# A sparse graph layer on one core: forms spread one to a block, three more units with a kept tile, short rows of A, and stores issued together with loads

## The chip, the cores and the metric

One core of a Trainium2 chip runs the kernel in one launch. The metric is the device time in microseconds (us) of one execution. The core has a matrix engine (PE; its weight loads are PEld), a vector engine (DVE), an activation engine (ACT), GpSimd (POOL) and SyncE (SP). Every engine works through its own queue of instructions in order. DMAs are issued from the queues of SP, ACT and POOL, and 16 DMA engines carry them out.

## The reference

`x` is 8 x 4096 x 256, `adj` is 4096 x 4096 (about 0.4% of its entries are nonzero, the low-numbered rows and columns most often), `W` is 256 x 256, all float32.

```python
HW = einsum('bnf,fo->bno', x, W)
A = relu((adj + adj.T) * 0.5)
D = sum(A, axis=1)
r = where(D > 0, D ** -0.5, 0)
L = eye(N) - r[:, None] * A * r[None, :]
out = relu(einsum('nm,bmo->bno', L, HW))
return layernorm(x + out, axis=-1)      # eps 1e-5, no scale or shift
```

## The kernel before

The work has two stages. The first makes a symmetric A in memory (`a_dram`), the degrees, the scaled products `g = r * (x W)` (`g_dram`, one row of 2048 floats, 8 KB, for each node, all eight batches side by side), and lists of which rows matter for which columns. The second, the gather stage, multiplies only the listed rows.

**First stage.** A is cut into 8 x 8 blocks of 512 x 512; A's 32 row groups have 128 rows each. The loop runs over rows `i` of blocks and, in each, over `j >= i`; a block off the diagonal handles (i,j) and (j,i) together. Per block: `load_adj` (SP queue, four buffers), transposes on PE and adds on DVE (`symmetrise`, L424 and L428), then ReLU on ACT, a sum per 64 columns on DVE (`part`, L433) and a store from the ACT queue (`keep`). After a row of blocks `degrees` gives r for its four row groups (L450 to L454). Beside a block's transposes PE does *forms*: `form(m, known)` loads x for row group m (two halves, `xin`), transposes it (L522) and multiplies by W (L533). A form is *known* when r of its rows is there: it is scaled and stored at once. The last ten row groups (`HOLD`) are formed *early*, kept in SBUF and scaled and stored by `release` later. From block row 4 on, the x loads of known forms go through the POOL queue. `multiply` adds each g's product with the first 128 columns of A to the result of the first row group (`lead`, L491). How many forms a block gets is set by a running `credit`: 1 for a block off the diagonal, 0.5 for one on it, doubled from row 4 on; in the last two block rows only the block on the diagonal gets one. Some blocks so get two forms and others none.

**Lists.** A unit u is a pair of row groups 2u+1 and 2u+2 (block 0 and block 1; the last unit has one). For each of the 4096 rows m a four-bit pattern says which of the four 64-column halves of the unit's columns have a nonzero there. `KINDS` are the patterns that have lists of their own (1, 2, 4, 8: one half; 3 and 12: one whole block; 5, 10, 9, 6: two halves of different blocks), and 0 stands for all the rest, treated as full. `CAPS[u]` gives the number of 128-row tiles of each kind. `patterns` makes the pattern; `count` (PE) and `place` (DVE) give each row a slot; `count_rest` and `place_rest` place what is left over; `spread` and `collect` turn slots into index lists, and `index` turns them into row numbers of `g_dram` (`gi`) and of a view of `a_dram` (`ai`, L385). The first four units of `SEQ` get theirs in the first stage, at times set in `due`; `spread` and `collect` are done there for the first two. In units in `HUB` the first 128 rows of g are not listed: they stay in an SBUF tile (`g_hub`), and only their part of A is loaded (L810).

**Gather stage.** For each unit in the order of `SEQ`, `steps_of` gives steps of one or two tiles. For each tile POOL issues two indirect DMAs: 128 pieces of A (`ga`, L815: 128 columns, or 256 when the tile touches both blocks) and 128 rows of g (`g`, L828, into a ring of 12 tiles, which is refilled when a step has used a tile). PE multiplies them into PSUM (L1033), four chunks of 512 columns, two passes each. Each block has four PSUM banks (tags b0 and b1). When a block is complete, `finish` has ACT evict it (L684), DVE add x (L694) and take mean and variance (L703 to L722); `normalise` (L727) follows later and then the store. Two of the b0 banks serve for the matmuls of `lists`, one step after block 0 of a unit is complete; DVE has to read them (L369, L370, L185 to L190) before the next unit can use these banks. The order on the queues is written out by hand: `queue(engine)` ties an instruction behind the last one of its engine, and `after(n, fn)` runs `fn` once steps worth n have passed (a step of two halves or one full block counts 2). x for a unit's two row groups is loaded on the ACT queue (`residuals`), 10 into the unit.

In `finish`, `rest` runs 1 after the block, and within it:

```python
def end():
    in_turn(normalise, i, z, mv, rstd)

after(3, end)
```

Of the kernel before, what the change touches and what calls it, by code (L numbers as in the profile page):

```python
# [9 lines left out]
F32 = mybir.dt.float32  # L10
# [13 lines left out]

OFFERS = [
# [9 lines left out]
SEQ = [1, 2, 3, 4, 5, 6, 7, 0, *range(8, 16)]  # L35

HUB = {0, 1, 3, 6, *range(8, 15)}
# [4 lines left out]
    [1, 3, 3, 2, 2, 1, 2, 2, 1, 1, 3],  # L42
    [1, 3, 3, 3, 2, 1, 1, 1, 1, 1, 2],
    [1, 3, 3, 2, 2, 2, 1, 1, 1, 1, 2],
    [1, 3, 3, 2, 2, 1, 1, 1, 1, 1, 2],
    [1, 3, 3, 2, 2, 1, 1, 1, 1, 1, 1],
# [13 lines left out]
def kernel(  # L60
# [28 lines left out]
    P = 128  # L89
# [15 lines left out]
    mid = KINDS.index(4), KINDS.index(5)  # L105
# [259 lines left out]
    def index(u, pl):  # L365
        t = tiles[u]

        low = ipool.tile([P, tmax], F32, tag="low", name=f"low_{u}")
        nc.vector.tensor_copy(low[:, :t], pl[:, 1, :])  # L369
        nc.vector.scalar_tensor_tensor(low[:, :t], pl[:, 0, :], float(P), low[:, :t], ALU.mult, ALU.add)  # L370
        gi = ipool.tile([P, tmax], U32, tag="gi", name=f"gi_{u}", bufs=3)
        nc.vector.tensor_scalar(gi[:, :t], low[:, :t], float(N), None, ALU.add)

        ai = ipool.tile([P, tmax], U32, tag="ai", name=f"ai_{u}", bufs=3)
        m0, m1 = first[u][mid[0]], first[u][mid[1]]
        if blocks(u) == 1:
            m0 = m1 = t
        for ts, n, k in (
            (slice(0, m0), NB, 2 * u + 1),
            (slice(m0, m1), NB, 2 * u + 2),  # L380
            (slice(m1, t), NU, u),
        ):
            if ts.start == ts.stop:
                continue
            nc.vector.tensor_scalar(  # L385
                ai[:, ts], low[:, ts], float(n), float(N * n + k), ALU.mult, ALU.add
            )
        plan[u] = gi, ai
        yield
# [9 lines left out]
    with (  # L399
# [173 lines left out]
        credit = 0.0  # L573
# [37 lines left out]

        for i in range(NS):
            diag = stat1.tile([P, A, P], F32, tag="diag", name=f"diag_{i}")
            for j in range(i, NS):
                tij = load_adj(i, j)
                tji = load_adj(j, i) if j > i else tij
                parts = [(i, j, tij, tji)] + ([(j, i, tji, tij)] if j > i else [])
                parts = [(p, spool.tile([P, A, S], F32, tag="sym", name=f"sym_{p[0]}_{p[1]}")) for p in parts]
                credit += (1.0 if j > i else 0.5) * (1 if i < 4 else 2)
                beside = [multiply(*args) for args in waiting]  # L620
                waiting.clear()
                products = len(beside)

                some = i < NS - 2 or i == j
                while some and credit >= 1.0 and (known or early):
                    beside.append(form(known.pop(0), True, i >= 4) if known else form(early.pop(0), False))
                    credit -= 1.0
                    some = i < NS - 2
                credit = min(credit, 1.0)
                for p, sym in parts:  # L630
                    for _ in symmetrise(*p, sym):
                        pass
                if i == NS - 1:


                    release_all(i - 1)
                    beside = beside[products:] + beside[:products]
                for n, b in enumerate(beside):
                    with tc.issue_after(done_pe[-1]) if i == NS - 1 and n < 2 else nullcontext():
                        for _ in b:  # L640
                            pass
                for (rows, cols, _, _), sym in parts:
                    keep(rows, cols, sym, diag)
                run_due()
            degrees(i)
            diags[i] = diag
            if i != NS - 2:
                release_all(i)
            known += range(i * A, min((i + 1) * A, NB - HOLD))
            if i == 1:  # L650
                for n, u in enumerate(SEQ[:2]):
                    patterns(u)
                    due += [[2 + n, count_place, (u,)], [4 + n, count_place_rest, (u,)]]
                due.sort(key=lambda d: d[0])
            elif i == 2:
                for n, u in enumerate(SEQ[2:4]):
                    patterns(u)
                    due.append([1 + n, count_place, (u,)])
                due.append([3, count_place_rest, (SEQ[2],)])
            elif i < 5 and i > 2:  # L660

                pieces = spread_early(SEQ[i - 3])
                for n in range(5):
                    due.append([1 + n // 2, next, (pieces, None)])
                due.append([4, collect_index, (SEQ[i - 3],)])
        run_due(True)
# [58 lines left out]
    def normalise(i, z, mv, rstd):  # L725
        for b in range(B):
            nc.vector.tensor_scalar(  # L727
                z[:, b, :],
                z[:, b, :],
                mv[:, b, 0:1],  # L730
                rstd[:, b : b + 1],
                ALU.subtract,
                ALU.mult,
            )
        nc.sync.dma_start(out[:, i * P : (i + 1) * P, :].rearrange("b p f -> p b f"), z)

    a_rows = a_dram.rearrange("j (c q) -> (j c) q", q=P)
    a_pairs = a_dram.rearrange("j (c q) -> (j c) q", q=2 * P)

# [29 lines left out]
    with (  # L769
# [3 lines left out]
    ):  # L773
        ring = [
# [3 lines left out]
        hub = gath.enter_context(tc.tile_pool(name="hub", bufs=1)).tile([P, G], F32, name="g_hub")  # L778
# [11 lines left out]
            "pool": mybir.EngineType.Pool,  # L790
        }
# [6 lines left out]
        def gather(n):  # L798
# [4 lines left out]
            both = len(targets(u, kind)) == 2  # L803
            at = apool.tile([P, 2 * P], F32, tag="a", name=f"ga_{u}_{t % tmax}")
# [9 lines left out]
            with queue("pool"):  # L814
                nc.gpsimd.indirect_dma_start(  # L815
                    out=at if both else at[:, :P],
                    out_offset=None,
                    in_=a_pairs if both else a_rows,
# [89 lines left out]
        def finish(i):  # L908

            if i == NB - 1:  # L910
                finish_last(i)
                return
# [3 lines left out]
            def rest():  # L916
# [6 lines left out]
                def end():  # L923
                    in_turn(normalise, i, z, mv, rstd)

                after(3, end)
# [3 lines left out]
        def residuals(rows):  # L930
# [61 lines left out]

        finish(0)
        side = None
        for q, (u, step) in enumerate(steps):
            new = q == 0 or steps[q - 1][0] != u
            last = q + 1 == len(steps) or steps[q + 1][0] != u
            if new:
                after(6, prepare, u)
                if q > 0:  # L1000
                    after(10 if u != SEQ[-1] else 4, residuals, range(2 * u + 1, 2 * u + 1 + blocks(u)))
# [9 lines left out]
            work = [(b, rows, *got[u, t]) for m in range(2) for k, t in step for b, rows in targets(u, k)[m : m + 1]]  # L1011
# [9 lines left out]
            for b, rows, at, gt in work:  # L1021
# [5 lines left out]
            for c in range(G // S):  # L1027
                for (b, rows, at, gt), new_rows in zip(work, fresh):
                    both = any(len(targets(u, k)) == 2 for k, t in step)
                    off = b * P if both else 0  # L1030
# [13 lines left out]
            run_later(sum(1 + (rows == slice(0, P)) for _, rows, _, _ in work))  # L1044
# [14 lines left out]
    with tc.If(short > 0):  # L1059
        with (  # L1060
# [4 lines left out]
            for i in range(NB):  # L1065
# [19 lines left out]
                normalise(i, z, mv, inverse_root(i, var, stat))  # L1085

# [27 lines left out]
```

## Time and profile before

| | |
|---|---|
| three runs | 1518.22, 1521.61, 1522.28 us; median 1521.61 |
| profiled execution | 1521.9 us, its span (first to last instruction) 1520.2 us, granted PE clock 0.982 |
| PE, DVE, POOL, ACT busy | 1437.9, 987.0, 693.6, 372.3 us |
| moved by DMA | 564.49 MB, 371 GB/s on average |
| L1033, products of gathered tiles | 2872 passes, 807.1 us busy; 176 more with the kept tile, 77.3 us |
| L828 and L815, the gathers | 268 each; 12.5 and 10.9 us from issue to landing |
| L735, stores of the result | 31 of 1 MB, 25.1 us from issue to landing |

The busy time of PE is modelled from the starts of matmuls, so a busy PE can still be short of its peak. The DMA share in the views is the mean busy share of the 16 DMA engines, and can stand slightly above 1. In brackets behind a row stands the idle time ahead of it and what ended it.

### The profile page before, as it was taken

How to read it: one execution, taken by the hardware profiler on the slowest of the kernel's cores; microseconds unless marked ns; L12 is line 12 of the kernel's file. 1: busy time of each engine (PE TensorE's matmuls, PEld its weight loads, DVE VectorE, ACT ScalarE, POOL GpSimd, SP SyncE). 2: the span in 40 equal slices, each digit the busy share in tenths (PEclk: the TensorE clock that was granted, in tenths of full speed). 3: DMA queues.
4: the chain of work that ended last, by engine and by line, in shares of the span. 5: the costliest groups of instructions: out<-in, count | busy, mean ns of one | idle time of the engine just before them, and what ended most of it. 6: DMA issues, size and time to landing. Idle time of an engine off the chain costs nothing.

```text
span 1520.2 us, 19332 instructions
## 1 busy us (share of the span) xinstructions
PE 1437.9 (95%) x6440; PEld 767.5 (50%) x6440; DVE 987.0 (65%) x3015; ACT 372.3 (24%) x462; POOL 693.6 (46%) x1051
## 2 busy tenths in 40 slices
PE   6999999989989989999999998999999999999994
PEld 5878877767767764433343333343433333333331
DVE  6576578898646362155659669579037888899533
ACT  3555554545434451010100100100010111001111
POOL 3002010010302225776767666666666767666652
PEclk9999999989999999999999999999999999999998
DMA  9999999999879998999999999999989999999995
GB/s 355 352 366 400 395 377 361 357 377 346 343 256 365 325 386 352 390 419 413 374 410 390 400 405 367 385 407 383 386 310 407 349 397 404 409 390 375 378 397 192
DMA packets 216713, 564.49 MB, mean 371 GB/s; under 512 B 16550, under 2 KB 104918, under 8 KB 180134
## 3 DMA queue, kind: packets, MB, share of 16 engines
q0 software_dynamic: 54224, 304.94, 50.6%
q1 hardware_dynamic: 93472, 126.89, 24.0%
q10 hardware_dynamic: 68912, 131.37, 22.8%
q8 instruction: 53, 0.87, 0.2%
q14 instruction: 52, 0.43, 0.1%
HBM read 443.61 MB, written 136.34 MB: 382 GB/s over the span
## 4 chain that ended last, share of the span: by engine, by line
PE 65%; DMA 17%; DVE 8%; issue 5%; ACT 2%; POOL 1%; ACTq 0%; SPq 0%; DVEq 0%; POOLq 0%
PE py L1033 45%; DMA g<-g_dram,gi 10%; PE pg L533 9%; PE lead L491 5%; DMA a_dram<-sym 4%; PE tr L424 3%; DVE sym L428 3%; PE xtr L522 3%; DVE part L433 2%; DMA ga<-a_dram,ai 2%; DMA xin<-in_x_dram 1%; ACT sym L432 1%; DMA adj<-in_adj_dram 1%; POOL ga L815 1%; PE lists L357 1%
## 5 line engine op out<-in xcount | busy, mean ns | idle before, releaser
L1033 PE MATMUL py<-g,ga 128*64 128x512 f32 (+1 forms) x2872 | 807.1, 597 | 16.4 <-DMA g<-g_dram,gi 14.2
L1033 PEld LDWEIGHTS py<-g,ga 128*64 128x64 f32 (+1 forms) x2872 | 293.8, 151 | 516.6 <-issue 487.2
L828 POOL DMA_INDIRECT g<-g_dram,gi x268 | 303.8, 1133 | 201.9 <-DMA g<-g_dram,gi 78.4
L815 POOL DMA_INDIRECT ga<-a_dram,ai x268 | 294.1, 1097 | 105.9 <-issue 77.7
L684 ACT ACTIVATE y<-py,minus_r 128x512 f32<-128x512 f32 x120 | 82.5, 687 | 799.7 <-PE py L1033 736.6
L694 DVE TENSOR_TENSOR xr<-xr,y 128x2048 f32<-128x2048 f32 x31 | 71.1, 2294 | 295.1 <-ACT y L684 294.5
L533 PE MATMUL pg<-w_sb,xt 128*128 128x256 f32 x1024 | 232.3, 385 | 5.2 <-ACT xt L523 5.2
L428 DVE TENSOR_TENSOR sym<-tr,adj 128x512 f32<-128x512 f32 x256 | 163.4, 682 | 101.5 <-PE tr L424 84.7
L533 PEld LDWEIGHTS pg<-w_sb,xt 128*128 128x128 f32 x1024 | 195.8, 194 | 33.5 <-ACT xt L523 5.6
L433 DVE TENSOR_REDUCE part<-sym 128x32 f32<-128x2048 f32 x64 | 145.4, 2278 | 63.2 <-ACT sym L432 63.2
L424 PE MATMUL tr<-ident,adj 128*128 128x128 f32 x1024 | 139.5, 287 | 28.7 <-DVE sym L428 14.6
L453 POOL TENSOR_TENSOR r<-e,neg_half 128x4 f32<-128x4 f32 x8 | 8.3, 1040 | 321.7 <-DVE e L452 239.6
L432 ACT ACTIVATE sym<-sym 128x2048 f32<-128x2048 f32 x64 | 122.6, 1916 | 128.0 <-DVE sym L428 109.4
L424 PEld LDWEIGHTS tr<-ident,adj 128*128 128x128 f32 x1024 | 119.9, 147 | 58.4 <-DVE sym L428 27.0
L522 PE MATMUL xtr<-ident,xin 128*128 128x128 f32 x512 | 73.7, 292 | 17.8 <-DVE sym L428 16.6
L703 DVE BATCH_NORM_STATS2 stats<-xr 128x6 f32<-128x256 f32 x256 | 87.0, 412 | 1.1
L727 DVE TENSOR_SCALAR xr<-xr,mv,root 128x256 f32<-128x256 f32 x248 | 84.2, 410 | 0.1
L491 PE MATMUL lead<-gt,strip 128*128 128x512 f32 x176 | 83.0, 598 | 0.0
L523 ACT COPY xt<-xtr 128x512 f32<-128x512 f32 x128 | 68.6, 591 | 48.1 <-PE xtr L522 47.3
L543 ACT ACTIVATE gt<-pg,r 128x512 f32<-128x512 f32 x88 | 60.6, 689 | 75.0 <-PE pg L533 72.3
L522 PEld LDWEIGHTS xtr<-ident,xin 128*128 128x128 f32 x512 | 60.8, 149 | 34.1 <-DVE sym L428 26.3
L1033 PE MATMUL py<-g_hub,ga 128*128 128x512 f32 x176 | 77.3, 592 | 0.0
(142 smaller groups left out, 836.8 us busy)
## 6 DMA issues: line engine op xcount, KB each, us to landing
adj<-in_adj_dram SPq DMA_DIRECT2D x64, 1024.0 KB, 10.6
a_dram<-sym ACTq DMA_DIRECT2D x64, 1024.0 KB, 9.4
out_dram<-xr SPq DMA_DIRECT2D x31, 1024.0 KB, 25.1
xr<-in_x_dram ACTq DMA_DIRECT2D x29, 1024.0 KB, 26.2
xin<-in_x_dram SPq DMA_DIRECT2D x44, 512.0 KB, 11.9
g_dram<-gt ACTq DMA_DIRECT2D x22, 1024.0 KB, 7.7
xin<-in_x_dram POOLq DMA_DIRECT2D x20, 512.0 KB, 5.8
g_dram<-held ACTq DMA_DIRECT2D x10, 1024.0 KB, 10.8
```

Of the source, the lines that this page charges most:

```text
L424: ins = nc.tensor.transpose(pt[:, c * P : (c + 1) * P], tji[:, c, a * P : (a + 1) * P], ident)
L428: nc.vector.tensor_add(sym[:, a, :], pt, tij[:, a, :])
L432: nc.scalar.activation(sym, sym, AF.Relu, scale=0.5)
L433: nc.vector.tensor_reduce(part[:, i * A : (i + 1) * A, j * S // Q : (j + 1) * S // Q], sym.rearrange("p a (c q) -> p a c q", q=Q), AX.X, A ...
L491: nc.tensor.matmul(lead[c], lhsT=strip, rhs=g[:, c * S : (c + 1) * S], start=not done, stop=len(done) == NB - 1, skip_group_check=True,)
L522: nc.tensor.transpose(pt[:, k, c, :], xin[b // H][:, b % H + k, c * P : (c + 1) * P], ident)
L533: ins = nc.tensor.matmul(pg[:, k * FO : (k + 1) * FO], lhsT=xt[:, b + k, c, :], rhs=w_sb[:, c, :], start=(c == 0), stop=(c == FC - 1),)
L703: nc.vector.bn_stats(stats[:, b, :], z[:, b, :])
L727: nc.vector.tensor_scalar(z[:, b, :], z[:, b, :], mv[:, b, 0:1], rstd[:, b : b + 1], ALU.subtract, ALU.mult,)
L815: nc.gpsimd.indirect_dma_start(out=at if both else at[:, :P], out_offset=None, in_=a_pairs if both else a_rows, in_offset=bass.IndirectOff ...
L828: nc.gpsimd.indirect_dma_start(out=gt, out_offset=None, in_=g_dram, in_offset=bass.IndirectOffsetOnAxis(ap=gi[:, t : t + 1], axis=0), boun ...
L1033: nc.tensor.matmul(py[2 * u + 1 + b][c][rows, :], lhsT=at[:, off + rows.start : off + rows.stop], rhs=gt[:, c * S : (c + 1) * S], start=ne ...
```

## The change

1. *Forms.* `credit` goes. One early form is placed ahead of the loop, and then `quota(i, j)` gives each block one form, except diagonal blocks of rows 0 to 3, which get none.
2. *Lists in the first stage.* Instead of two units after block row 1 and two after row 2, one unit each starts after rows 1, 2, 3 and 4; the left-over rows of the fourth are placed in the gather stage, as before.
3. *Hub.* Units 2, 4 and 5 join `HUB`; each gives up one gathered tile (unit 2 one of kind 0, unit 4 one of kind 12, unit 5 its one of kind 6). The hub tile's place in SBUF moves ahead of the ring.
4. *Short rows.* For kinds 1, 2, 4 and 8 only the 64 columns in question are fetched from A (256 bytes a row in place of 512); `index` makes the numbers kind by kind.
5. *Order.* Unit 0 comes after unit 9 instead of after unit 7.
6. *Stores and loads.* `normalise` follows directly in `rest`. The store is put off: `exchange` issues the oldest finished store on SP together with the x load of one row group on ACT, at 6 and at 12 into each unit (2 and 4 in the last).

```diff
-SEQ = [1, 2, 3, 4, 5, 6, 7, 0, *range(8, 16)]
-HUB = {0, 1, 3, 6, *range(8, 15)}
+ALONE = {1, 2, 4, 8}
+SEQ = [*range(1, 10), 0, *range(10, 16)]
+HUB = {*range(7), *range(8, 15)}
 CAPS = [
...
-    [1, 3, 3, 2, 2, 1, 2, 2, 1, 1, 3],
+    [1, 3, 3, 2, 2, 1, 2, 2, 1, 1, 2],
     [1, 3, 3, 3, 2, 1, 1, 1, 1, 1, 2],
-    [1, 3, 3, 2, 2, 2, 1, 1, 1, 1, 2],
     [1, 3, 3, 2, 2, 1, 1, 1, 1, 1, 2],
+    [1, 3, 3, 2, 2, 1, 1, 1, 1, 0, 2],
...
-        for ts, n, k in (
-            (slice(0, m0), NB, 2 * u + 1),
-            (slice(m0, m1), NB, 2 * u + 2),
-            (slice(m1, t), NU, u),
-        ):
...
+        for k, kind in enumerate(KINDS):
+            if not CAPS[u][k]:
+                continue
+            ts = slice(first[u][k], first[u][k] + CAPS[u][k])
+            if kind in ALONE:
+                n, at = N // Q, 2 * (2 * u + 1) + kind.bit_length() - 1
...
+            nc.vector.tensor_scalar(ai[:, ts], low[:, ts], float(n), float(N * n + at), ALU.mult, ALU.add)
...
-        credit = 0.0
+        def quota(i, j):
+            if i in (2, 3) and j == i:
+                return 0
+            return int(j > i or i > 3)
...
+        for _ in form(early.pop(0), False):
+            pass
         for i in range(NS):
...
-                while some and credit >= 1.0 and (known or early):
-                    beside.append(form(known.pop(0), True, i >= 4) if known else form(early.pop(0), False))
-                    credit -= 1.0
+                for _ in range(quota(i, j)):
+                    if known:
+                        beside.append(form(known.pop(0), True, i >= 4))
+                    elif early:
+                        beside.append(form(early.pop(0), False))
...
-            if i == 1:
-                for n, u in enumerate(SEQ[:2]):
-                    patterns(u)
-                    due += [[2 + n, count_place, (u,)], [4 + n, count_place_rest, (u,)]]
...
+            if i in (1, 2, 3, 4):
+                u = SEQ[i - 1]
+                patterns(u)
+                due.append([2, count_place, (u,)])
+                if i < 4:
+                    due.append([4, count_place_rest, (u,)])
...
-                    out=at if both else at[:, :P],
-                    in_=a_pairs if both else a_rows,
+                    out=at if both else at[:, :Q] if half else at[:, :P],
+                    in_=a_pairs if both else a_halves if half else a_rows,
...
-                def end():
-                    in_turn(normalise, i, z, mv, rstd)
-                after(3, end)
+                in_turn(normalise, i, z, mv, rstd)
+                finished.append((i, z))
...
-        def residuals(rows):
+        def exchange(rows):
+            if finished:
+                with queue("sp"):
+                    store(*finished.pop(0))
             for i in rows:
                 with queue("act"):
                     xr[i] = residual(i, nc.scalar)
...
-                    after(10 if u != SEQ[-1] else 4, residuals, range(2 * u + 1, 2 * u + 1 + blocks(u)))
+                after(6 if u != SEQ[-1] else 2, exchange, rows[:1])
+                if q > 0:
+                    after(12 if u != SEQ[-1] else 4, exchange, rows[1:])
```

## The prediction

> **What bounds it now.** I read the stages first (windows view: length, busy time of PE, PEld, DVE, ACT and POOL with instruction counts, granted clock, DMA share, GB/s).
>
> ```profile
> 0.00:222.00 222.00, 202.68 (x1167) 169.99 (x1168) 141.56 (x173) 116.78 (x141) 28.56 (x403) 0.99 1.03 373
> 222.00:383.50 161.50, 145.06 (x785) 112.47 (x783) 140.03 (x393) 75.20 (x84) 8.10 (x17) 0.96 0.99 362
> 383.50:546.00 162.50, 150.83 (x815) 117.46 (x816) 88.74 (x128) 73.58 (x88) 38.80 (x63) 0.96 0.88 325
> 546.00:595.50 49.50, 44.14 (x133) 24.22 (x132) 15.73 (x29) 16.56 (x16) 15.47 (x22) 0.93 0.93 367
> 595.50:905.00 309.50, 309.50 (x1213) 119.37 (x1214) 186.98 (x705) 24.43 (x36) 216.76 (x197) 1.00 1.01 400
> 1139.00:1338.00 199.00, 199.00 (x852) 76.34 (x851) 162.57 (x636) 22.83 (x34) 135.15 (x119) 1.00 1.00 392
> ```
>
> Rows i=0,1 of the first stage (to 222) are bound by transfers (share 1.03). Rows 2,3 (to 383.5) nearly so, with VectorE at 140 of 161.5. Rows 4 to 6 (to 546) leave transfers idle (0.88). In the gather stage (595.5 to 1507) PE and the DMA engines are both full. Which leads? I counted the matmuls of L1033 off against the steps of each unit. A pass of 512 columns is due 0.43 us (the chain has PE lead L491 x72 in 30.9 us); two half-width passes into different column halves share one slot. That gives 2000 slots, 857 us, in a stage of 911.7. The other 54.7: the lists' matmuls 17.6; waits for gathers 25.3 (13.5 in units 6, 7 and 0, between 917 and 1045; 11.8 in unit 15); one wait for VectorE 2.2; the rest, small, 9.6. The chain of waits (start, length) leaves PE for gathers in those places only:
>
> ```profile
> 854.20 50.40 PE py L1033 x184
> ...
> 904.87 12.37 DMA g<-g_dram,gi
> ...
> 1456.57 13.38 DMA g<-g_dram,gi
> ```
>
> So PE leads, and transfers add 25 us. Then the boundary between two units, on the timeline (start, length):
>
> ```profile
> 1230.49 2.29 DVE L694 TENSOR_TENSOR xr<-xr,y 128x2048 f32<-128x2048 f32 x1 [5.41 <-ACT y L684]
> 1233.55 0.95 PE L357 MATMUL lists<-val,hot 128*128 128x28 bf16 x32
> 1238.62 0.17 DVE L369 COPY low<-lists 128x14 f32<-128x14 f32 x1
> 1239.43 0.31 DVE L385 TENSOR_SCALAR ai<-low 128x5 uint32<-128x5 f32 x3
> 1241.14 0.52 DVE L189 TENSOR_TENSOR pos_k<-incl_k,lists 128x352 f32<-128x352 f32 x1
> 1242.13 2.84 DVE L727 TENSOR_SCALAR xr<-xr,mv,root 128x256 f32<-128x256 f32 x8
> ```
>
> VectorE reads the lists out of two of the four b0 banks, and only then normalises. Unit 10's first step begins at 1241.3 and needs the first of these banks for its third column chunk, 1.7 us later; L189 frees it at 1241.7. The spare time is 1.4 us. At unit 12 it is negative already, and PE waits:
>
> ```profile
> 1341.53 1.94 PE L1033 MATMUL py<-g,ga 128*64 128x512 f32 x8 [2.01 <-DVE pos_k L189]
> ```
>
> **First stage: forms and lists.** All 32 forms stay. A form is 8.7 us of PE (xtr x16 1.75, pg x32 6.91), its product 3.4. Rows 0,1: one form goes ahead of the loop and K0 leaves block (1,1); the bytes before row 2 are the same at a share of 1.03, so 0. (That form's loads stand first on SP and hold the first adj back by 1 MB, about 2.7 us; its own PE work covers them, and they would cost that if it didn't.) The time from a block's first L428 to the next block's is 15.5 on average for (1,2) to (1,6), one form each. In (2,3) to (2,5), with a place or a rest behind the form, it is 19.0, 18.7 and 18.3: about 3 more. Rows 2,3 lose two of four places and one of three rests: I take two at 3.2, 6 us gained. Rows 4 to 6 have nine forms before and after, but before they stand as 2,2,0,0 / 2,2,0 / 1,0: 27.0 and 27.9 in the off-diagonal blocks with two, 7.3 to 14.0 in those with none, 162.6 in all. With one per block: three diagonal blocks at 14 (PE: 8.7+3.4+1.75 of transposes), six others at 15.5, 135; the two places and one rest that arrive, 3.2+3.2+2.8; and the two lists' spreads (each 7 us of VectorE: hot, inn, val), now beside fuller blocks, half counted, 8. Sum 152: 10 gained. Bounds: 18 gained with all arrivals hidden, 7 lost as in rival 2. Last row: one product (3.4) moves behind (6,7); PE has gaps at 550 to 560, so I take 2 lost. On POOL the xin loads from row 4 on stay as many and in order. Net -14.
>
> **Three hub units.** Units 2, 4 and 5 each lose a gathered tile (16, 8 and 8 slots) and gain the kept one (16 each): 16 slots more, +6.9 us of PE. Counted in the reference's inputs, 32174 listed rows become 31798: 376 x 8 KB, 3.1 MB less. Leftover rows (233, 135, 193) fit their room of 256, so the full pass stays unused. The A tiles balance. Prices from the page (packets, MB, share of the span): 2.5 us a MB on q0, 2.9 on q1, 2.6 on q10. The gain is 7.8 us of transfer.
>
> ```profile
> q0 software_dynamic: 54224, 304.94, 50.6%
> q1 hardware_dynamic: 93472, 126.89, 24.0%
> q10 hardware_dynamic: 68912, 131.37, 22.8%
> ```
>
> On POOL three pairs of gathers (1.10+1.13) go and three loads of 0.59 come: not on the path.
>
> **Short rows.** 145 tiles fetch 32 KB instead of 64. In the trace's packet records a packet of eight 512-byte rows takes 159 ns and one of a single 8-KB row 309: rows of 512 B cost no more than their bytes. By bytes, 145 x 0.033 MB x 2.5 = 12 us less. The Trainium skill speaks against it: "DMA: Bandwidth & Descriptors" asks in Specifications for at least 512 B, with a read-modify-write below that, and in "Why small descriptors are slow" counts 11 cycles for a descriptor of 256 B, not 8. No row here is below 512 B, so this trace can't decide. By 11 against 19 cycles the saving is 10 (an estimate); with the time per byte doubled it is 0. I take 10, nearest to the trace; ends 12 gained and 24 lost (four times the byte price).
>
> **Order of units.** Unit 0 (102.8 us of PE for 26 tiles) lets the ring of 12 refill. It goes behind units 8 and 9, whose transfers (54 and 51 us at the prices above) leave PE's 52 and 50 no spare. No instruction is added.
>
> **VectorE at the boundary.** normalise now comes ahead of the lists' reads: 8 instructions, 2.8 us. index has up to 11 ai instructions instead of 3, issued 0.08 us apart: 0.6. The read ends 3.4 later, and the new unit's products queue behind it on PE. The spare time is 1.4 to 2.0 at units 3, 6, 7, 0, 9, 10 and 11; at unit 5 it falls from 4.7 to 1.3, since unit 4 loses a full-width step of 3.4 behind its block 0; at 2, 4 and behind unit 0 it is above 4. Eight boundaries therefore wait about 2.0, and unit 12 waits 3.4 more: +19. Bounds 0 and 27.
>
> **Stores and loads.** As many of 1 MB as before. SP has nothing behind a store that waits for normalise. A load on ACT reuses a buffer whose store went out a unit earlier (over 45 us; landing takes 25), so the evictions behind it don't wait: 0, bounds -3 and +3.
>
> **Gather stage.** The waits up to unit 0, 13.5, stand against 7.8 less transfer, 6.9 more PE and some 14 us of bank waits. The tail's 11.8 stand against 5.4 of bank waits, 4 of short rows and 2 from units 8 and 9. I leave 2; what is late next is VectorE. Sum: 864 + 17.6 + 9.6 + 2.2 + 19 + 2 = 914, against 911.7: +3.
>
> Total: 1521.9 (the profiled execution; its span is 1520.2) - 14 + 3 = 1511. The median, 1521.6, is 0.3 below it.
>
> **Rivals.** 1 (0.17), faster: the banks don't hold PE, the reads starting earlier than I count. The stage is 864+17.6+9.6+2.2+4 = 897, the total 1494. For it: one such wait exists now. Against: VectorE's order is written out in the code.
> 2 (0.17), slower: the places that move to rows 4 and 5 stand where PE has no slack. A place is 12 us of VectorE (1240.2 to 1242.2 and 1246.8 to 1256.6 at the boundary above). If it holds the next block's L428 for all of it, rows 4 to 6 take 170 and lose 7, and the total is 1528; it decides from 9 us a place. For it: VectorE's 140 in rows 2,3. Against: places there cost 3.
> 3 (0.09): short rows at four times the byte price. Waits for gathers are then 25.3+24-7.8-6.9-19 = 16, not 2, and the total 1525.
> 4 (0.07): the forms stay bunched in issue order, whatever the quota says; with the stage's +3 lost again elsewhere, 1519 to 1523.
> The remaining 0.50 is the forecast, 1500 to 1522 by its bounds.
>
> **Numbers.** A measurement of this kernel tells about 0.3%, 4.6 us, from no change. Faster: 0.42 of the forecast, rival 1, and 0.03 of the others, 0.62. Same: 0.06 of the forecast, 0.05 of rival 4, 0.04 of the others, 0.15. Slower 0.23. The range is 1493 to 1528, from rival 1 to rival 2.
>
> **What would show it.** Right: rows 4 to 6 near 152 us with a share above 0.93; L1033 waiting for DVE pos_k at some nine unit starts, about 2 us each; waits for gathers under 5 us. Wrong: one such pos_k wait as now, or rows 4 to 6 no shorter.

## The result: 0.45% less time, and the profile after

Five runs of the changed kernel have a median of 1512.71 us (1512.4 to 1516.33), five of the kernel before 1520.52 (1518.22 to 1522.28). The ratio is 0.9955, with a 95% interval from 0.9939 to 0.997: faster by 7.8 us, a little more than the 0.3% that this measurement can tell from nothing. The forecast was 1511. The profiled execution took 1512.47 us, its span 1510.8, against 1521.9 and 1520.2.

The stages first (windows view of the changed kernel; columns as in the prediction: length, busy time of PE, PEld, DVE, ACT, POOL, granted clock, DMA share, GB/s). The cuts are moved to this kernel's own stage ends.

```profile
0.00:222.00 222.00, 203.71 (x1169) 169.88 (x1169) 139.76 (x173) 116.65 (x141) 28.56 (x403) 0.98 1.02 377
222.00:375.70 153.70, 137.30 (x760) 108.84 (x759) 120.70 (x273) 74.14 (x83) 11.62 (x22) 0.96 1.01 372
375.70:533.20 157.50, 150.14 (x833) 115.90 (x832) 117.98 (x277) 73.02 (x90) 37.15 (x61) 0.98 0.94 347
533.20:580.70 47.50, 44.57 (x140) 23.92 (x138) 9.28 (x16) 16.58 (x17) 15.20 (x21) 1.00 0.93 377
580.70:914.00 333.30, 329.69 (x1301) 128.82 (x1302) 200.87 (x777) 27.42 (x40) 233.47 (x207) 1.00 0.98 379
1236.00:1480.00 244.00, 237.23 (x956) 90.62 (x955) 175.26 (x682) 28.04 (x42) 165.39 (x143) 0.99 0.99 384
```

The reader is to see two things. In rows 2,3 VectorE falls from 140 to 121 us, and in rows 4 to 6 it rises from 89 to 118 while the DMA share goes from 0.88 to 0.94: the places moved, and the stage got shorter. In the gather stage the opposite: PE had no gap in the two stretches of it that the prediction shows (309.5 and 199.0 us, which leave out the waits of the kernel before), and now has gaps of 3.6 and 6.8 us in the two longer stretches shown here, 5.1 of the 6.8 at unit 12. The gather stage starts at 580.7 instead of 595.5 and lasts 917 us instead of 911.7.

What PE waits for there is told by the waits view (PE, 595 to 1500 us; total, number, longest). Before, this answer had waits for gathers, and one wait for pos_k, which VectorE makes from the lists' matmuls:

```profile
PE py L1033 <- DMA g<-g_dram,gi: 14.2, 8, 3.4
PE py L1033 <- DVE pos_k L189: 2.0, 1, 2.0
```

Now it has one line:

```profile
PE py L1054 <- DVE pos_k L190: 18.4, 9, 5.1
```

The chain of waits (start, length) has PE alone in the tail, where the prediction showed 13.38 us of a gather at 1456:

```profile
1381.89 45.33 PE py L1054 x160
...
1428.01 68.01 PE py L1054 x252
```

The boundary in front of unit 11 shows how the wait comes about (timeline: start, length, engine, in brackets the idle time and what ended it):

```profile
1284.19 2.69 DVE L729 TENSOR_SCALAR xr<-xr,mv,root 128x256 f32<-128x256 f32 x8
1286.80 0.16 DVE L370 COPY low<-lists 128x14 f32<-128x14 f32 x1
1286.91 0.37 SPq L739 DMA_DIRECT2D out_dram<-xr  x1
1287.11 1.24 ACTq L680 DMA_DIRECT2D xr<-in_x_dram  x2
1287.60 0.74 DVE L388 TENSOR_SCALAR ai<-low 128x1 uint32<-128x1 f32 x10
1289.75 0.52 DVE L190 TENSOR_TENSOR pos_k<-incl_k,lists 128x352 f32<-128x352 f32 x1
1290.32 4.08 PE L1054 MATMUL py<-g,ga 128*64 128x512 f32 x18 [1.63 <-DVE pos_k L190]
```

normalise (L729) now ends before the first read of the lists, the ten ai instructions stand in the middle, and L190, which reads the first of the two banks last, frees it at 1290.3, 3.4 us after normalise; PE is 1.63 us late. At unit 12 the same wait is 5.14 us:

```profile
1342.06 1.98 PE L1054 MATMUL py<-g,ga 128*64 128x512 f32 x4 [5.14 <-DVE pos_k L190]
```

The queues (packets, MB, share of 16 engines' span) answer to the three of the prediction: only q0 changed, by 7.8 MB.

```profile
q0 software_dynamic: 53808, 297.17, 50.1%
q1 hardware_dynamic: 93472, 126.89, 24.0%
q10 hardware_dynamic: 68912, 131.37, 22.7%
```

### The profile page after: what moved, and what is told of

Same layout as the page of the kernel before. It is cut to its first block, busy times and chain, and to the rows that moved or that the text cites. A ratio compares the mean times of both kernels' runs of the same rounds, so it can differ in the third digit from the quotient of the medians.

```text
span 1510.8 us, 19483 instructions
## 1 busy us (share of the span) xinstructions
PE 1434.3 (95%) x6448; PEld 763.6 (51%) x6448; DVE 997.9 (66%) x3134; ACT 370.6 (25%) x462; POOL 717.9 (48%) x1048
## 4 chain that ended last, share of the span: by engine, by line
PE 63%; DVE 14%; DMA 13%; issue 5%; POOL 2%; ACT 2%; ACTq 0%; DVEq 0%; POOLq 0%
PE py L1054 38%; PE pg L534 11%; PE lead L492 6%; DMA g<-g_dram,gi 5%; DMA a_dram<-sym 4%; PE tr L425 4%; PE xtr L523 3%; DVE sym L429 3%; DMA ga<-a_dram,ai 2%; DVE stats L705 1%; DVE xr L696 1%; POOL ga L822 1%; POOL g L835 1%; DVE part L434 1%; DVE xr L729 1%
## 5 line engine op out<-in xcount | busy, mean ns | idle before, releaser
L1054 PE MATMUL py<-g,ga 128*64 128x512 f32 (+1 forms) x2832 | 790.2, 598 | 18.4 <-DVE pos_k L190 18.4
L1054 PEld LDWEIGHTS py<-g,ga 128*64 128x64 f32 (+1 forms) x2832 | 286.3, 150 | 508.8 <-issue 461.8
L835 POOL DMA_INDIRECT g<-g_dram,gi x265 | 329.9, 1245 | 198.6 <-PE py L1054 87.3
L822 POOL DMA_INDIRECT ga<-a_dram,ai x265 | 290.7, 1097 | 94.2 <-issue 70.5
L425 PE MATMUL tr<-ident,adj 128*128 128x128 f32 x1024 | 136.2, 281 | 22.4 <-DVE sym L429 13.1
L425 PEld LDWEIGHTS tr<-ident,adj 128*128 128x128 f32 x1024 | 116.0, 143 | 53.6 <-DVE sym L429 29.0
L1054 PE MATMUL py<-g_hub,ga 128*128 128x512 f32 x224 | 98.4, 592 | 0.0
L482 POOL DMA_DIRECT2D xin<-in_x_dram x20 | 15.1, 757 | 165.1 <-PE xtr L523 165.1
L729 DVE TENSOR_SCALAR xr<-xr,mv,root 128x256 f32<-128x256 f32 x248 | 84.6, 413 | 1.1
```

The costliest lines, as they stand in the source:

```text
L425: ins = nc.tensor.transpose(pt[:, c * P : (c + 1) * P], tji[:, c, a * P : (a + 1) * P], ident)
L729: nc.vector.tensor_scalar(z[:, b, :], z[:, b, :], mv[:, b, 0:1], rstd[:, b : b + 1], ALU.subtract, ALU.mult,)
L822: nc.gpsimd.indirect_dma_start(out=at if both else at[:, :Q] if half else at[:, :P], out_offset=None, in_=a_pairs if both else a_halves if ...
L835: nc.gpsimd.indirect_dma_start(out=gt, out_offset=None, in_=g_dram, in_offset=bass.IndirectOffsetOnAxis(ap=gi[:, t : t + 1], axis=0), boun ...
L1054: nc.tensor.matmul(py[2 * u + 1 + b][c][rows, :], lhsT=at[:, off + rows.start : off + rows.stop], rhs=gt[:, c * S : (c + 1) * S], start=ne ...
```

## The experiments

The experiments ran on four chips, on which the kernel before took 1519 to 1528 us, so kernels are compared by their ratio to the kernel before on the same chip, and stages by their traces. A difference between traces of two chips can hold some us of the chips. The first four kernels below ran on the slowest (1528 us), where neither the kernel before nor the changed one has a trace; the pages of these traces give no times of landing, so a wait for a gather may stand there under "issue", that is, without a cause. The theory that was to be tested: the first stage gives some 14 us, and the two PSUM banks, read behind normalise, give much of it back.

### The order on VectorE: undone, and done alone

Reads first: the changed kernel with normalise behind the reads, as before.

```diff
-                in_turn(normalise, i, z, mv, rstd)
-                finished.append((i, z))
+                def end():
+                    in_turn(normalise, i, z, mv, rstd)
+                    finished.append((i, z))
+                after(3, end)
```

> The changed kernel with one part undone: normalise stands again behind the reads of the lists. Theory (the two b0 banks hold PE at nine unit starts): PE's waits for DVE pos_k fall from 18.4 us to about 3 (unit 12 alone), waits for gathers rise to 2 to 4, total 1512.7 - 14 = 1498 to 1500. Rival (transfers lead as soon as PE is quicker): the waits for gathers come back to 10 or more, total 1506 or above. Second rival (the late read only shifts idle time): no difference, 1511 to 1514.

Measured: 0.987 (0.9853 to 0.9887), so 0.9915 of the changed kernel, 13 us less. The wait for pos_k falls from 18.4 us in nine places to one:

```profile
PE py L1057 <- DVE pos_k L190: 4.2, 1, 4.2
```

The gather stage takes 908.6 us instead of 917. That is 8.4 of the 13 us; the traces do not show the rest, since that of the changed kernel is of a faster chip (1520.5 us for the kernel before, against 1528), and the first stage, not edited here, was 4 us longer in this one. Eight of the nine waits went. Unit 12's stayed: it took 53.8 us, as in the changed kernel (53.7), and in front of it VectorE now has no idle time, with an earlier normalise (from 1320.53) ahead of the moments (from 1323.12). And new waits came: unit 3 took 66.5 us instead of 64.6, unit 2 69.0 instead of 67.9. The waits view has 2.8 us in these two units under "issue"; that they are gathers is likely, but not shown.

Normalise first: the kernel before with the same one edit the other way round.

```diff
-                def end():
-                    in_turn(normalise, i, z, mv, rstd)
-
-                after(3, end)
+                in_turn(normalise, i, z, mv, rstd)
```

> The kernel before with this one part added: normalise directly behind the inverse root, so ahead of the reads. The reads end 2.8 us later. Theory: seven boundaries with 1.4 to 2.0 of spare time wait about 1.3 us each and unit 12 waits 2.8 more, 12 us of new waits for pos_k; but here PE also waits 25 us for gathers, and a slower PE asks for them later: some 8 to 10 of those vanish, so the total is only 2 to 4 above before. Rival (the waits add up whatever stands beside them): 12 above. Third: the earlier normalise lets stores and loads go earlier and is worth something by itself: at or below before.

Measured: 1.0038 (1.0019 to 1.0057), 5.8 us more, above the expected 2 to 4.

```profile
PE py L1030 <- DVE pos_k L189: 11.8, 5, 4.9
```

Beside this line the view has 1.1 us for another read of the lists and 8.2 without a cause. The stage grew from 911.7 to 920.4 us, between traces of two chips. In the tail, unit 15, PE's waits fell from 12.5 us to 0.4: PE was held at the banks so long that the gathers were no longer late. So a bank wait isn't paid in full while transfers are late elsewhere.

### The short rows of A: undone, with and without the bank waits

Both kernels fetch 128 columns of A for every tile again; the second also has normalise behind the reads. The row numbers in `index` and the offsets in the products follow this line:

```diff
-            half = kind in ALONE
+            half = False
```

> The changed kernel with whole rows of A (128 columns) for kinds 1, 2, 4 and 8 again; ai then has fewer different formulas but as many instructions. 4.75 MB more, 12 us of transfer. Theory (PE is held by the banks, transfers have room): waits for gathers stay under 4, total 1512.7 to 1515. Rival (transfers still lead): 8 to 12 more, 1521 to 1525. Rival (a row of 256 B costs as much as one of 512 B): no difference, and q0's share of the engines equal.

Measured: 0.9978 (0.9963 to 0.9992), beside 0.9955 of the changed kernel: 3.5 us worse, with intervals that overlap. In the trace the stage takes 925.8 us instead of 917, more than the ratio allows (again two chips): unit 6 takes 2.6 us longer and unit 7 4.0, with 3.3 us of waits in the stage without a cause in the view.

> Both of the above: normalise behind the reads and whole rows of A. Theory: once the banks don't hold PE, the 12 us of transfer count in part: waits for gathers 8 to 12, total 5 to 9 above the kernel with the reads first and short rows, about 1504 to 1508. Rival (a short row is no cheaper than a whole one): equal to it.

Measured: 0.9863 (0.9845 to 0.988), the same as 0.987 with the short rows. The gather stage takes 908.7 us, against 908.6 on the same chip with the short rows. The expected loss of 5 to 9 us did not come: it was a miss of mine, and the short rows are worth between nothing and some 3.5 us of time, although they take 4.7 MB off q0.

### The banks, read ahead of everything that nobody waits for

Here and in the next two kernels the changed kernel was run again beside them, to have one chip for all.

> The changed kernel itself, unedited, so that the other three and it are timed side by side. 0.995 to 0.996 of the kernel before.

Measured: 0.9956 (0.9942 to 0.9969), span 1509.7 us.

Reads before the root: the lists are read right behind the moments, and gi and ai are computed only after the reads.

```diff
+        yield
         gi = ipool.tile([P, tmax], U32, tag="gi", name=f"gi_{u}", bufs=3)
...
         plan[u] = gi, ai
-        yield
...
-                with queue("dve"):
-                    rstd = inverse_root(i, var, stat)
-                in_turn(normalise, i, z, mv, rstd)
-                finished.append((i, z))
+                def end():
+                    with queue("dve"):
+                        rstd = inverse_root(i, var, stat)
+                    in_turn(normalise, i, z, mv, rstd)
+                    finished.append((i, z))
+                after(3, end)
...
+                if not last and 2 in ahead[u]:
+                    in_turn(run, reads[0])
```

> The changed kernel, with the lists read out of the two b0 banks right behind the moments of a row, ahead of its inverse root and of normalise, and gi and ai computed only after those reads. Theory (the banks hold PE): the wait for pos_k is 0 at every unit, unit 12 included, where normalise behind the reads still left 4 to 6; the changed kernel minus 17 to 20 us, so about 0.983 of the kernel before. Rival (what is left at unit 12 comes from the moments being late, not from the order behind them): the same as with normalise behind the reads, 0.987.

Measured: 0.9856 (0.9834 to 0.9878); against the changed kernel on the same chip 0.99, 15 us, a little short of the expected 17 to 20. The profiled execution, the fastest of its five, is 18.4 us of span shorter (1491.3). PE (waits view, 580 to 1478 us) no longer waits for VectorE at any boundary:

```profile
PE py L1059 <- DMA g<-g_dram,gi: 2.2, 1, 2.2
```

The boundary in front of unit 11 (timeline) has the last two reads of the banks, L190 and L191, ahead of gi, ai, the root and normalise:

```profile
1268.44 0.52 DVE L190 TENSOR_TENSOR pos_k<-incl_k,lists 128x352 f32<-128x352 f32 x1
1269.00 0.52 DVE L191 TENSOR_TENSOR pos_k<-pos_k,lists 128x352 f32<-128x352 f32 x1
1269.58 0.73 DVE L389 TENSOR_SCALAR ai<-low 128x1 uint32<-128x1 f32 x10
1272.77 2.69 DVE L729 TENSOR_SCALAR xr<-xr,mv,root 128x256 f32<-128x256 f32 x8
```

Unit 11 begins at 1271.8, so the banks are free 2 us ahead of it. The gather stage takes 897.7 us, 19.3 less than the changed kernel's on this chip (917.0). The rival, that what was left at unit 12 came from late moments and not from the order behind them, fell: unit 12 does not wait either.

Counted off against the steps, the units of the two kernels differ in the nine that had waited and in the tail, and in no other by 0.1 us. The nine take 24.2 us less (unit 12 7.7, unit 0 3.9, the others 1.3 to 2.2), and unit 15, where PE waits for a gather again, takes 4.9 more: 19.3. So a late bank cost PE more than the 18.2 us of idle time that the waits view of the changed kernel has on this chip.

### The first stage: its two parts alone

Forms only: the kernel before with the quota and the form ahead of the loop (the diff of the section on the change, without the lists).

> The kernel before with one part of the change: the quota of one form per block and the one form ahead of the loop; the places, the boundary, the kept tiles and the rows of A as before. Theory: rows 4 to 6 of the first stage shorten by about 10 us, because no place or spread arrives there beside the even forms; rows 2 and 3 stay at 161; the gather stage stays at 912; 0.993 to 0.995 of the kernel before. Rival (the 5 us that rows 4 to 6 gained in the changed kernel is all that even forms give, and the other part of the gain was the lists'): 5 us, 0.997.

Measured: 1.0003 (0.9987 to 1.0019), no gain at all. Both the theory and its rival missed.

Lists only: the kernel before with one unit's lists per row.

> The kernel before with the other part of the first stage alone: one unit's lists per row, so that two places and a rest leave rows 2 and 3 for rows 4 and 5. Theory: rows 2 and 3 shorten by 6 us, rows 4 to 6, still with two forms in their first blocks, take 3 to 9 us more; between -3 and +3 us in all, 0.998 to 1.002. Rival (the places cost nothing in rows 4 to 6, since transfers and PE leave room there): -6 us, 0.996.

Measured: 1.0044 (1.0027 to 1.0061), 6.7 us slower. Rows 2,3 gained 5.5 of their 6 us, but rows 4 to 6 lost 11, more than the expected 3 to 9.

So neither part gains by itself, and both together gain 14.8 us of first stage. From the first sym add of each row, in us:

| kernel | rows 2,3 | rows 4 to 6 | last row and tail | gather stage starts |
|---|---|---|---|---|
| before | 161.7 | 162.6 | 49.4 | 595.5 |
| lists only | 156.2 | 174.0 | 48.2 | 599.3 |
| forms only | 161.3 | 166.9 | 49.2 | 594.7 |
| changed | 155.0 | 157.5 | 47.5 | 580.7 |

Rows 0,1, which are the rest, took 221.8, 220.9, 217.3 and 220.7. The waits of VectorE in rows 4 to 6 name both losses. Of lists only:

```profile
DVE incl_k L185 <- PE tot L227: 28.7, 2, 16.2
```

The counts that a place starts from are products on PE, queued behind two bunched forms; VectorE takes its work in order, so the next sym add, and PE's transposes behind it, wait as well. Of forms only, where no place stands in these rows:

```profile
DVE sym L428 <- DMA a_dram<-sym: 19.9, 4, 9.5
```

VectorE waits for the store of a sym tile, whose buffer the next block takes. The timeline of block (4,6) in forms only tells why it comes late (ACTq is ScalarE issuing a DMA):

```profile
413.35 2.48 DVE L428 TENSOR_TENSOR sym<-tr,adj 128x512 f32<-128x512 f32 x4 [6.73 <-DMA a_dram<-sym]
...
415.87 1.91 ACT L432 ACTIVATE sym<-sym 128x2048 f32<-128x2048 f32 x1 [5.31 <-DVE sym L428]
...
419.96 1.91 ACT L432 ACTIVATE sym<-sym 128x2048 f32<-128x2048 f32 x1 [2.18 <-DVE sym L428]
...
422.08 1.56 ACT L523 COPY xt<-xtr 128x512 f32<-128x512 f32 x3 [0.22 <-PE xtr L522]
...
423.40 0.37 ACTq L439 DMA_DIRECT2D a_dram<-sym  x1
...
433.84 2.48 DVE L428 TENSOR_TENSOR sym<-tr,adj 128x512 f32<-128x512 f32 x4 [9.53 <-DMA a_dram<-sym]
```

The first relu ends at 417.8, but its store is issued at 423.4, behind the second relu and the form's xt copies. In the chain of waits (start, length) it then takes until 433.65, and the first add of the next block starts at 433.84, 20.5 after this one's:

```profile
423.40 10.25 DMA a_dram<-sym
```

The same block in the changed kernel:

```profile
411.01 0.68 DVE L429 TENSOR_TENSOR sym<-tr,adj 128x512 f32<-128x512 f32 x1
...
414.53 1.92 ACT L433 ACTIVATE sym<-sym 128x2048 f32<-128x2048 f32 x1 [4.42 <-DVE sym L429]
...
416.48 0.37 ACTq L440 DMA_DIRECT2D a_dram<-sym  x1
417.40 2.06 ACT L524 COPY xt<-xtr 128x512 f32<-128x512 f32 x4 [0.95 <-PE xtr L523]
```

Here the store goes out as soon as its relu ends, 5.5 us after the first add instead of 10. ScalarE's instructions stand in another order. In the first stage the two kernels differ in nothing but the lists, so the lists' work in these rows must have brought the other order about; how is not shown. ScalarE's order in block (4,6), by start:

```
forms only    relu  relu  xt xt xt  store  xt  gt gt gt  store  gt
changed       relu  store  xt xt xt xt  relu  gt gt  store  gt gt
```

Whether the late store is the cause was put to the test directly.

### The stores of sym ahead of the forms

Forms only, with `keep` of a block (relu, the sum per 64 columns and the store) written ahead of its forms in rows 4 to 6. ScalarE's order becomes relu, store, relu, xt, store, xt xt xt, gt gt gt gt.

```diff
+                if 4 <= i < 7:
+                    for (rows, cols, _, _), sym in parts:
+                        keep(rows, cols, sym, diag)
                 ...
                 for n, b in enumerate(beside):
                 ...
-                for (rows, cols, _, _), sym in parts:
-                    keep(rows, cols, sym, diag)
+                if not (4 <= i < 7):
+                    for (rows, cols, _, _), sym in parts:
+                        keep(rows, cols, sym, diag)
```

> The kernel with even forms alone, with one edit more: in rows 4 to 6 the relu and the store of a block's sym tiles are written ahead of the forms, so that ScalarE's issue order puts them before or among the xt copies and no longer behind the gt evictions. Theory (with even forms alone rows 4 to 6 took 166.9 us because VectorE's next add waited 19.9 us for the store of the sym tile whose buffer it reuses, and that store stood behind the form's evictions on ScalarE): that wait goes below 3 us, rows 4 to 6 take 135 to 150 us, and the kernel 0.98 to 0.99 of the kernel before. Rival (PE's own work, a form, a product and the transposes, sets these blocks, and the stores only look late): rows 4 to 6 stay at 160 or more, ratio 1.00.

Measured: 0.9882 (0.9864 to 0.9901), against 1.0003 without the edit. Rows 4 to 6 take 149.7 us instead of 166.9 (windows view, forms only first, then VectorE's wait with the edit in the same window):

```profile
378.60:545.50 166.90, 152.06 (x827) 118.06 (x825) 97.67 (x132) 73.11 (x90) 36.80 (x61) 0.96 0.89 328
384.10:533.80 149.70, 146.27 (x826) 114.05 (x825) 97.58 (x133) 75.82 (x91) 39.19 (x61) 1.00 0.98 366
```

```profile
DVE sym L428 <- DMA a_dram<-sym: 6.7, 5, 2.2
```

The wait went from 19.9 to 6.7 us (below 3 was expected), the longest from 9.5 to 2.2, and PE is busy for 146 of 150 us. So the place of relu and store in ScalarE's queue is the cause; the two moved together, and the wait that fell is the one for the store. Even forms with early stores make these rows 13 us shorter than before (162.6). How much of that early stores would give with the forms bunched as before was not tried. There VectorE waits once for a store in these rows, 7.0 us, and 50.4 us for transposes (waits view, 383.5 to 546).

The same edit on the changed kernel with reads before the root:

> The changed kernel with the lists read ahead of the inverse root, and the same edit of the stores in rows 4 to 6. Theory: rows 4 to 6 fall from 158 to 145 to 150 us, since the two places and the rest still stand there; the gather stage stays at 897; 0.978 to 0.981 of the kernel before. Rival (the places already put the stores early in this kernel, so nothing is left to gain): 0.9856, as without the edit.

Measured: 0.9825 (0.9802 to 0.9848). That lies between the forecast and its rival, and the interval overlaps that of the kernel without the edit (0.9834 to 0.9878). The trace speaks for the rival, that nothing is left to gain: rows 4 to 6 take 160.8 us, not 145 to 150, and the gather stage starts at 583.0 instead of 580.6. The longest of VectorE's waits in 370 to 535 us is this:

```profile
DVE low L370 <- PE pl L358: 17.2, 1, 17.2
```

That is block (6,6), 24.6 us long, where PE works through the products left over, a form and then pl. But forms only with early stores has this wait too (14.5 us, in a block of 21.7), so it explains 3 of the 11 us that these rows take longer here (160.8 against 149.7). The others lie in rows 4 and 5, where in this kernel the two places and a rest still stand: (5,7) is 4.2 us longer, (4,6) and (5,6) 2.5 each, (4,5) 1.3, and (4,7) 2.8 shorter, and VectorE waits 6.7 us for the counts of the places and 3.4 for those of the rest. So the lists were put back to rows 2 and 3:

```diff
-            if i in (1, 2, 3, 4):
-                u = SEQ[i - 1]
-                patterns(u)
-                due.append([2, count_place, (u,)])
-                if i < 4:
-                    due.append([4, count_place_rest, (u,)])
+            if i == 1:
+                for n, u in enumerate(SEQ[:2]):
+                    patterns(u)
+                    due += [[2 + n, count_place, (u,)], [4 + n, count_place_rest, (u,)]]
+            elif i == 2:
+                for n, u in enumerate(SEQ[2:4]):
+                    patterns(u)
+                    due.append([1 + n, count_place, (u,)])
+                due.append([3, count_place_rest, (SEQ[2],)])
```

> The changed kernel with the lists read ahead of the inverse root, the stores of the sym tiles ahead of the forms in rows 4 to 6, and the lists' places again where the kernel before had them, in rows 2 and 3. Theory (with the stores early the places in rows 4 and 5 hide behind nothing: rows 4 to 6 took 160.8 us with them and 149.7 without): rows 2 and 3 take 162, rows 4 to 6 150, the gather stage begins at 579 and takes 897; a span of 1488 to 1490, 0.979 to 0.982 of the kernel before. Rival (a place costs the same wherever it stands, 6 us in rows 2 and 3 and as much in rows 4 and 5): the gather stage begins at 583 as without this edit, 0.9825.

Measured: 0.9799 (0.9778 to 0.9821), 1488.96 us, the fastest of all. Rows 2,3 take 161.5 us, rows 4 to 6 149.7 and the gather stage 897.9, as expected; it begins at 576.3, earlier than the expected 579.

```profile
220.00:381.50 161.50, 140.80 (x776) 110.71 (x775) 142.51 (x402) 74.50 (x85) 11.29 (x22) 0.96 0.99 359
381.50:531.20 149.70, 146.38 (x827) 114.15 (x825) 98.54 (x148) 75.83 (x91) 38.95 (x61) 1.00 0.98 366
531.20:576.30 45.10, 44.87 (x140) 23.96 (x138) 9.29 (x16) 14.71 (x16) 13.72 (x20) 1.00 0.92 374
576.30:1473.00 896.70, 894.28 (x3553) 344.45 (x3553) 598.95 (x2371) 84.27 (x123) 591.48 (x538) 1.00 0.99 383
```

PE is busy for 894 of 897 us in the gather stage. By ratio the step from the kernel with the moved lists is 0.0026 with overlapping intervals. The traces are 6.7 us apart where the gather stage begins, but on two chips; forms only with early stores, whose first stage has this order too, begins it at 578.9 on the chip of the moved lists, 4.1 us ahead of them. So the traces speak for this order, by 4 to 7 us.

### The three kept tiles, undone

Reads before the root, with HUB and CAPS of before (the order of units stays new).

> The changed kernel with the lists read ahead of the inverse root, and the kept tiles as before: units 2, 4 and 5 gather their tile again, 6.9 us less of matmuls and 3.1 MB more of gathers, 7.8 us of transfer. Theory (with VectorE out of the way the stage is bound by PE, and 10 us more of transfer was absorbed when the short rows were undone): 3 to 7 us faster than 0.9856, so 0.981 to 0.9835. Rival (the kept tiles pay for themselves because the transfers of units 2 to 8 are the limit once PE has no gaps): waits for gathers of 5 us and more come back at units 5 to 8, and the time is equal or up to 5 us slower, 0.9856 to 0.989.

Measured: 0.9861 (0.9842 to 0.988), equal to 0.9856. The gather stage takes 904.0 us instead of 897.7, although PE has 6.9 less to do, and PE waits for gathers (580 to 1500 us):

```profile
PE py L1059 <- DMA g<-g_dram,gi: 7.5, 9, 2.5
```

Counted off against the steps, units 4 and 5 take 3.3 and 3.4 us less, but unit 7 takes 7.3 more, units 6, 9 and 0 1.2 to 1.8 each, and the tail 1.3. The other two kernels with the reads moved and the new kept tiles have stages of 895.5 (on this chip) and 897.9, so 904.0 is hardly one trace's chance, though the ratios do not tell the two apart. My theory fell and its rival held: the tiles that PE multiplies in addition are paid for by gathers that are not late.

## Why the prediction was right

- Rows 0,1, at nothing, and rows 2,3, at 6: measured 1.1 and 6.7 us. The count of places and rests that leave was right, and lists only shows it alone (5.5).
- Rows 4 to 6, at 10: measured 5.1. This is the term that was mis-sized. Its base, 135 us by PE's work and 143 with the two lists' spreads, left out the stores: forms only, with no place arriving, took 166.9. Only with the stores early did they come near it, 149.7: (4,4) and (5,5) took 14.8 and 13.5, the six off-diagonal blocks 16.6 on average, and (6,6), with three products in it, 21.7. The places and the rest, charged at 9, cost 11 with the stores early (160.8 against 149.7). That the changed kernel does better than forms only, 157.5 against 166.9 in spite of that work, goes with the order on ScalarE, which the sum didn't have at all: VectorE's waits for stores of sym are 5.6 us there (375.7 to 533.2) against 19.9. So it was in part luck that these rows gained at all: the step that the sum rests on, one form to a block, lost 4 us here when it stood alone.
- Tail, at +2: measured -2; in the windows PE's gaps there fell from 5.4 to 2.9 us. First stage, at -14: measured -14.8. The sum is nearer than its parts by luck: rows 4 to 6 gave 5 less than forecast, the tail 4 more.
- VectorE at the boundary, at +19, eight boundaries of 2.0 and unit 12: the trace has eight (units 3, 5, 6, 7, 8, 9, 0, 11), of 1.1 to 2.1 us, and unit 12, 5.1. The prediction's list has 10 in place of 8: it took the spare times in the old order, but the long unit 0 now stands ahead of 10, which does not wait, and no longer ahead of 8. In all 18.4 us in nine waits against 2.0 in one, so +16.4; by the lengths of the units, measured against the kernel that reads ahead of the root, 24.3 against 2.2, so +22. Undoing the order gave 13 us back, reading ahead of the root 15. The cause is shown, and the forecast of its size lies between these two numbers.
- Waits for gathers, at 2 left: PE's waits view shows none, and unit 15 has 0.4 us over its slots. That they would go because PE is held was right: with normalise first the tail's 12.5 us also went, without any other part of the change; with the bank waits gone 5 us of it returned.
- Three hub units, at +6.9 of PE and -7.8 of transfer: about even in the ratio, and worth 6 us of the stage in the traces, once the reads were moved; in the changed kernel itself they were not undone.
- Short rows, at -10 of transfer: the row first. In the packet records of the changed kernel a packet of eight 256-byte rows takes 84 ns, one of eight 512-byte rows 159, a single 8-KB row 309: 75 ns for every 2 KB, and 9 for the packet. So 256-byte rows cost little but their bytes: 75 ns less for each of 145 tiles on every engine, 10.9 us (an estimate), about the 10 that the prediction took. The rule of the Trainium skill's "DMA: Bandwidth & Descriptors", Specifications (at least 512 B, a read-modify-write below), would have made these rows dearer and does not show; for these gathers into SBUF the measurement decides. Its section "Why small descriptors are slow" charges the 11 cycles instead of 8 to a packet, and says that putting consecutive descriptors into one packet spreads this overhead; the trace agrees, with one fixed part for eight rows, where the prediction charged every row. In time the short rows were worth some 3.5 us at most.
- Stores and loads, at nothing: the trace agrees, as far as it goes. The store on SP goes out when normalise ends (1286.91) and both loads together at the unit's start (1287.11), so the pairing at steps 6 and 12 is not seen in time. This part, and the new order of units, were not tried alone.
- Gather stage, at 914: measured 917. Total, at 1511: 1512.7.

Rival 1, that the banks don't hold PE, was wrong of this kernel, but its sum, a stage of 897, is what the kernel took when the reads were moved ahead (897.7). Rival 2 is what happens with the lists moved and the forms left bunched: rows 4 to 6 at 174 us, for the reason that rival gave, places where VectorE holds the next block. In the changed kernel, with even forms and its order on ScalarE, it did not come about. Rival 3 fell with the 84 ns. Rival 4 fell too: the off-diagonal blocks of rows 4 to 6 take 15.7 to 21.3 us, where they took 7.3 to 27.9.

## What to carry to other kernels

Two edits that gain nothing, or lose, one by one can gain together, as even forms and moved lists did here: a part's share is known only when it is run alone and with the others. A DMA that a compute engine issues waits for its turn in that engine's order (here 5.6 us behind its tile's last write), and the buffer behind it with it: compare the time at which a tile is last written with the time at which its store is issued. At a stage's end, read first what frees a bank or a buffer for the next one, and leave what only ends in a store for later.

## What the hardware showed that was not expected

Gathered rows of 256 bytes cost hardly more per byte than rows of 8 KB: 84 ns for a packet of 2 KB, 42 ns per KB, against 309 ns for 8 KB, 39 per KB. And the gaps of PE in the profile fell short of what late banks cost: 18.2 us of gaps, in nine units that were 24.2 us longer.
